# A graph layer's gathers: fewer buffers, later release in the start, and end parts placed by hand

## The chip, the cores and the metric

One core of a Trainium2 chip runs the whole program. The metric is the time of one execution on the device in microseconds, as the median over several runs; lower is better. The engines are TensorE (PE, with its weight loads as PEld), VectorE (DVE), ScalarE (ACT), GpSimd (POOL) and SyncE (SP). SP does no arithmetic here; it issues DMAs. POOL does nothing but issue indirect DMAs, the gathers.

## The reference, cut to what matters

```python
# x: 12500 x 64; src, dst: 200000 (sorted by dst); edge_attr: 200000 x 64; dist: 200000 x 1
nodes = x[stack([src, dst], 1)].reshape(200000, 128)
gates = (ssp(edge_attr @ We1 + be1) @ We2 + be2) * (1 - sigmoid(5 * (dist - 3.5)))
h     = ssp(nodes @ Wn1 + bn1) @ Wn2 + bn2
sums  = zeros_like(x).at[dst].add(h * gates)
new   = x + ssp(sums @ Ws1 + bs1) @ Ws2 + bs2
out   = layernorm(x + new)          # ssp(v) = softplus(v) - log 2, all in float32
```

## The kernel before, in words

The edges are cut into 391 groups of 512. For each group the kernel needs the rows `x[src]` of its edges. Four gathers on POOL bring them, 128 rows each, into a buffer `xg` (`gather`, L183). In twelve groups SP fetches the last 128 rows one by one instead (`fetch`, L198), so those groups have three gathers. The other half of a node product, `x[dst] @ Wn1`, is not gathered: since the edges are sorted by `dst`, the destinations of 256 edges lie within 42 neighbouring nodes, and the kernel first writes a table of all nodes' products to HBM and later loads 42 rows of it (`load`, L211). One-hot columns (`onehot`, L216), written by DVE into the same `xg` buffer, pick the right row.

**The start.** POOL issues the gathers of the first groups at once; `src` is the only thing that they need. Meanwhile constants and the transposed `x` are loaded. Then the table is made in 14 pieces: for each, PE multiplies (L501), ACT and DVE each copy a part from PSUM to `tb` (L503, L504), SP stores it, DVE clears a part of `sums` (L506). PE has two PSUM buffers for the pieces, so it is at most two ahead of the copies. After each piece stands one call of `gather(g, after=True)`: DVE writes one element of the `xg` buffer (L178), and POOL's gather of that group must wait for that write. Engines work through their queues in the order of the program, so a gather that waits holds back all later gathers, and nothing else.

**The loop.** The order of the work is written by hand (`tc.manual_schedule()`); each engine takes its own instructions in this order. In iteration i, PE does the first part of layer 2 for group i-1 (L266, L269), layer 1 for group i+1 (L233, L235, L241), the scatter of group i-3 (L292), the transposes of group i+3 (L224) and the rest of layer 2 for group i-1 (L275). ACT does exponential and logarithm of group i+1 (L252, L255) and copies the transposed rows (L229). DVE multiplies the messages (L284, L288), adds the scattered sums into `sums` (L308), takes the softplus (L260) and writes one-hots. SP loads group i+5 and fetches single rows. POOL's part is one call, `gather(i + AHEAD - 1)`. The pool has `AHEAD + 5` = 25 buffers `xg`. A gather can go as soon as its buffer is free, and that is when the scatter of the group 25 before has been done by PE; POOL, which has no other work, then takes it at once.

**Node blocks.** Whenever the sums of a block of 512 nodes are complete, its output is computed in ten parts (`node_block`): fetch of `x`, `hidden` with `clamp`, `logs`, `center`, `ssp`, `layer2` with `add`, `square`, `variance`, `root`, `scale`, `store`. `BLOCK_STEPS` says how many iterations after completion each part stands; the third row is for a block that completes close to the end.

**The end.** From iteration `ends = last - CATCH_UP` on, the loop has another branch: transposes are done for the next group only, and twice a later stage does two groups in one iteration (`second`, `third`), so that the pipeline runs empty. The last two groups and the last block follow the loop in an order written out by hand.

Of the kernel before, what the change touches and what calls it, by code (L numbers as in the profile page):

```python
# [42 lines left out]
F32 = mybir.dt.float32  # L43
# [19 lines left out]
PIECES = 3  # L63
NB = 512
K = 4
AHEAD = 20
LOADS = 5
SPREADS = 5
CATCH_UP = 17
PREPARE = 5  # L70

BLOCK_STEPS = ((2, 3, 4, 4, 6, 7, 8, 9, 10, 14), (2, 3, 3, 4, 5, 6, 7, 8, 9, 10), (1, 1, 1, 2, 3, 3, 4, 4, 4, 4))
ROWS = 4
CUTOFF = 5.0
EPS = 1e-5
# [28 lines left out]
def gnn_resnorm_kernel(ctx: ExitStack, tc: tile.TileContext, a: dict, out: bass.AP, E: int):  # L104
# [67 lines left out]

    def gather(g, after=False):

        xg = loads.tile([P, K, P], F32, name="xg", bufs=AHEAD + 5)
        xgs[g] = xg
        if after:
            nc.vector.memset(xg[:, 0, :1], 0.0)  # L178
        for k in range(K - (g in by_rows)):
            if padding(g, k):  # L180
                nc.vector.memset(xg[:, k, :D], 0.0)
                continue
            nc.gpsimd.indirect_dma_start(  # L183
                out=xg[:, k, :D], out_offset=None, in_=x,
                in_offset=bass.IndirectOffsetOnAxis(ap=src_i[:, g, k : k + 1], axis=0))
# [68 lines left out]
    def logs(g, part=every):  # L254
        nc.scalar.activation(us[g][:, part], us[g][:, part], AF.Ln, bias=one)  # L255
# [47 lines left out]
    def window(g):  # L303
        if g not in window_at:
            window_bases(g)
        for h in range(2):
            part = sums[h * D : (h + 1) * D, bass.ds(window_at[g][h], W)]
            nc.vector.tensor_add(part, part, scs[g][h * D : (h + 1) * D, h * W : (h + 1) * W])  # L308
# [89 lines left out]
    with tc.manual_schedule():  # L398
# [4 lines left out]
        with tc.tile_pool(name="prep", bufs=1) as prep:  # L403
# [15 lines left out]
            nc.sync.dma_start(dist, a["dist_l"])  # L419
            dst_i = rel.bitcast(I32)  # L420
            nc.sync.dma_start(dst_i.rearrange("p g k -> p (g k)"), a["dst_l"])
            FREE = AHEAD - 2 * PARTS
            for g in range(FREE):
                gather(g)

            nc.vector.memset(one, 1.0)
            nc.vector.memset(half, 0.5)
# [68 lines left out]
            for i in range(PARTS):  # L496
                for c in range(i * CP, (i + 1) * CP, CP // 2):
                    m = CP // 2
                    ps = z_tile().rearrange("p b (k f) -> p (b k) f", k=K)
                    for k in range(m):  # L500
                        nc.tensor.matmul(ps[:, k, :], xT[:, c + k, :], wnb, start=True, stop=True)  # L501
                    tb = prep.tile([P, m, 2 * D], F32, name="tb", bufs=6)
                    nc.scalar.copy(tb[:, :K, :], ps[:, :K, :])  # L503
                    nc.vector.tensor_copy(tb[:, K:, :], ps[:, K:m, :])  # L504
                    nc.sync.dma_start(by_node[:, c : c + m], tb)
                    nc.vector.memset(sums[:, c * P : WIDE if c + m == NCH else (c + m) * P], 0.0)  # L506
                    gather(FREE + c // m, after=True)
                if i == 1:
                    nc.vector.tensor_copy(base_i, base_b[:1])
                    for k in range(2):  # L510
                        nc.vector.tensor_copy(be3[:, k, :], rows[:, 0, :])
                    for k in range(K):
                        nc.vector.tensor_copy(row3[:, :, k, :], rows[:, 1:3, :])
                        nc.vector.tensor_copy(rs3[:, k, :], rows[:, 3, :])
                if i == 2:
                    nc.vector.tensor_copy(rel, dst_i)
                    for t in range(2):
                        r = rel[:, :, 2 * t : 2 * t + 2]
                        nc.vector.tensor_sub(r, r, base_b[:, :NH].rearrange("p (g h) -> p g h", h=2))


        with tc.tile_pool(name="finish", bufs=1) as finish:
# [5 lines left out]
            def lagging(i, lag, steps):  # L528

                lag -= sum(i > step for step in steps)  # L530
                return [g for g in range(i - lag, i - lag + 1 + (i in steps)) if g >= 0]

            for i in range(-3, NG):
                second[i] = lagging(i, 1, (ends + 5,))
                third[i] = lagging(i, 3, (ends - 2, ends + 8))
                ahead[i] = [i + 3] if i < ends else [i + 2] if i == ends + 1 else [i + 1] if i > ends + 2 else []
            parts, begun, complete = {}, None, 0

            def at(f, g, *more):
                if 0 <= g < NG:  # L540
                    f(g, *more)
# [5 lines left out]
            for i in range(-3, last - 1):  # L547
                now = parts.pop(i, [])
                early = [part for part in now if part.tensor]
                at(load, i + LOADS)  # L550
                fetch(i)
                if i > 0:
                    at(gather, i + AHEAD - 1)
                if i < ends:
                    for g in second[i]:
                        layer2_edge(g)
                    if i >= -1:
                        zs[i + 1] = z_tile()
# [12 lines left out]
                    for g in second[i]:  # L571
                        layer2_node(g)
                    for g in second[i]:
                        hcut(g)
                        message(g)
                    for g in third[i]:
                        window(g)
                    for part in early:
                        part.others()
                    at(softplus, i + 1)  # L580
                else:
                    for g in ahead[i]:
                        transposes(g)
                        xcopy(g)
                    zs[i + 1] = z_tile()
                    layer1_edge(i + 1)
                    for part in early:
                        part.tensor(zs[i + 1][:, 1, HE:])
                    layer1_node(i + 1)
                    exps(i + 1)  # L590
                    logs(i + 1)
                    for g in second[i]:
                        layer2(g)
                        hcut(g)
# [12 lines left out]
                complete = third[i][-1] + 1 if third[i] else 0  # L607
                if blocks and complete >= blocks[0][1] - PREPARE and not begun:
                    begun = node_block(*blocks[0][0], finish)
                    begun.pop(0).others()  # L610
                if blocks and complete >= blocks[0][1]:
                    steps = next(steps for steps in BLOCK_STEPS if i + steps[-1] < last - 1)
                    for n, part in zip(steps, begun, strict=True):
                        parts.setdefault(i + n, []).append(part)
                    blocks.pop(0)
                    begun = None
            assert len(blocks) == 1 and begun and not parts
# [8 lines left out]
            for some in (edge, node):  # L626
                exps(last, some)
                logs(last, some)
            for g in range(last - 2, last + 1):
                window_bases(g)  # L630
            layer2(last - 1)
# [5 lines left out]
            scatter(last - 1, tx_tile()[:, : 2 * W])  # L637
            softplus(last, node)
            window(last - 2)
            layer2_node(last)  # L640
            window(last - 1)
            hcut(last)
            message(last)
            scatter(last, tx_tile()[:, : 2 * W])
            window(last)
            for part in begun:
                node_part(part)

# [146 lines left out]
```

## Time and profile before

| | us |
|---|---|
| median of 3 runs | 2539.01 |
| lowest, highest | 2535.73, 2542.47 |
| the profiled execution's own time | 2535.25 |
| its span, from the first to the last instruction | 2533.4 |
| mean granted TensorE clock in it | 0.866 |

The profile's page gives for each group of instructions its line, engine, output and input, count, busy time, mean duration and the idle time ahead of it with what ended it. The timeline gives the start, the duration, the engine and line, and in brackets how long the engine had been idle and who released it; "remote" and "issue" are cases in which the trace names nobody. Row counts (x4) say that neighbouring equal instructions were merged. Tables by stretch give, for each engine, busy time and count, then the granted clock, the share of the DMA engines in use and GB/s.

### The profile page before, as it was taken

The numbers are of one execution on the slowest core, as the hardware profiler recorded it, in microseconds if no ns is written. First come the engines' busy times: TensorE is split into PE (matmuls) and PEld (weight loads), VectorE is DVE, ScalarE is ACT, GpSimd is POOL, SyncE is SP. The second block draws the span as 40 slices with busy tenths as digits, with TensorE's granted clock in tenths as the row PEclk, the third lists the DMA queues.
The fourth block names the chain that finished last, engine by engine and source line by source line (L and its number), as shares of the span: only waits on it lengthen the run. The fifth ranks groups of instructions, "written<-read, shape, count | busy, mean of one in ns | idle before, by whom it ended". The sixth has DMA issues, their size and how long they took to land. (4 is left out here: it accounts for less than half of the span.)

```text
span 2533.4 us, 41076 instructions
## 1 busy us (share of the span) xinstructions
PE 2139.0 (84%) x11373; PEld 1735.4 (69%) x11373; DVE 1085.8 (43%) x2745; ACT 920.1 (36%) x1317; POOL 1469.2 (58%) x1555
## 2 busy tenths in 40 slices
PE   4569888988988888888879987988898889888897
PEld 3457676777767767667767766766777667766775
DVE  3224434444444444444444444444444444444553
ACT  1123333333333333333333433333434333333442
POOL 6655666666666666656666655566666666666400
PEclk9998889788888888888997888888888888899895
DMA  7312222222222222222222222222222222222210
GB/s 194 90 45 52 51 50 53 51 51 53 51 55 50 53 52 55 53 52 57 51 55 56 50 53 53 52 57 52 57 54 53 56 54 57 55 61 55 54 48 8
DMA packets 170982, 143.07 MB, mean 56 GB/s; under 512 B 46475, under 2 KB 142915, under 8 KB 170746
## 3 DMA queue, kind: packets, MB, share of 16 engines
q1 hardware_dynamic: 119746, 87.95, 12.0%
q0 software_dynamic: 49632, 50.92, 11.2%
q8 instruction: 93, 1.52, 0.3%
q10 hardware_dynamic: 1368, 1.51, 0.2%
q14 instruction: 143, 1.17, 0.1%
HBM read 130.57 MB, written 9.63 MB: 55 GB/s over the span
## 5 line engine op out<-in xcount | busy, mean ns | idle before, releaser
L183 POOL DMA_INDIRECT xg<-in_x,src_i x1551 | 1469.0, 947 | 919.4 <-issue 361.1
L252 ACT ACTIVATE u<-z 128x768 f32<-128x768 f32 x392 | 317.0, 809 | 1435.7 <-PE z L241 469.1
L284 DVE TENSOR_TENSOR h<-gh,cut 128x256 f32<-128x256 f32 x391 | 165.9, 424 | 1162.9 <-PE z L241 369.9
L241 PE MATMUL z<-xT,wns 106*128 106x256 f32 x1564 | 497.2, 448 | 7.1 <-issue 3.2
L275 PE MATMUL gh<-consts,s 128*128 128x64 f32 x3128 | 428.9, 284 | 7.0 <-issue 6.9
L269 PE MATMUL gh<-consts,s 128*128 128x128 f32 x1564 | 310.5, 326 | 141.7 <-issue 124.1
L275 PEld LDWEIGHTS gh<-consts,s 128*128 128x128 f32 x3128 | 423.6, 210 | 4.8 <-issue 4.8
L241 PEld LDWEIGHTS z<-xT,wns 106*128 106x128 f32 x1564 | 353.1, 228 | 78.7 <-issue 8.5
L269 PEld LDWEIGHTS gh<-consts,s 128*128 128x128 f32 x1564 | 229.0, 211 | 248.7 <-issue 222.7
L260 DVE SCALAR_TENSOR_TENSOR s<-u,z 128x768 f32<-128x768 f32 x392 | 372.7, 951 | 47.6 <-issue 26.2
L255 ACT ACTIVATE u<-u,one 128x768 f32<-128x768 f32 x392 | 365.9, 933 | 12.7
L224 PE MATMUL tx<-consts,xg 128*106 128x128 f32 x1552 | 278.4, 307 | 62.8 <-ACT u L255 29.4
L235 PE MATMUL z<-eT,consts 128*128 128x256 f32 x782 | 314.7, 489 | 0.0
L292 PEld LDWEIGHTS z<-xg,msg 128*128 128x128 f32 x1484 | 272.0, 227 | 47.5 <-issue 16.1
L292 PE MATMUL z<-xg,msg 128*128 128x84 f32 x1484 | 257.0, 298 | 21.1 <-issue 20.7
L224 PEld LDWEIGHTS tx<-consts,xg 128*106 128x106 f32 x1552 | 209.9, 160 | 86.6 <-issue 38.2
L229 ACT COPY xT<-tx 106x512 f32<-106x512 f32 x391 | 221.4, 566 | 35.9 <-PE tx L224 18.5
L308 DVE TENSOR_TENSOR sums<-sums,z 64x42 f32 x742 | 145.8, 197 | 129.1 <-issue 113.9
L288 DVE TENSOR_TENSOR msg<-gh,h 128x256 f32<-128x256 f32 x391 | 165.9, 424 | 13.4
L235 PEld LDWEIGHTS z<-eT,consts 128*128 128x128 f32 x782 | 131.9, 212 | 54.9 <-issue 16.1
L266 PE MATMUL gh<-row,ones 3*128 3x512 bf16 x391 | 156.9, 401 | 3.3 <-issue 2.5
L216 DVE TENSOR_TENSOR xg<-consts,rel 128x168 f32<-128x168 f32 x391 | 135.9, 348 | 0.2
(100 smaller groups left out, 635.7 us busy)
## 6 DMA issues: line engine op xcount, KB each, us to landing
eT<-in_eT SPq DMA_DIRECT2D x391, 128.0 KB
xg<-in_x,src_i POOLq DMA_INDIRECT x1551
xr<-in_x SPq DMA_DIRECT2D x1536, 0.2 KB
wns<-table SPq DMA_DIRECT2D x782, 21.0 KB
table<-tb SPq DMA_DIRECT2D x14, 448.0 KB
sums<-in_xT SPq DMA_DIRECT2D x7, 455.0 KB
y<-in_x SPq DMA_DIRECT2D x24, 128.0 KB
out<-y SPq DMA_DIRECT2D x24, 128.0 KB
```

Of the source, the lines that this page charges most:

```text
L183: nc.gpsimd.indirect_dma_start(out=xg[:, k, :D], out_offset=None, in_=x, in_offset=bass.IndirectOffsetOnAxis(ap=src_i[:, g, k : k + 1], ax ...
L224: nc.tensor.transpose(tx[:, k, :], row, ident)
L229: nc.scalar.copy(xT, xTs[g])
L235: nc.tensor.matmul(zs[g][:, 0, :HE], we1.rearrange("a h d -> a (h d)"), eTs[g], start=False, stop=True, skip_group_check=True)
L241: nc.tensor.matmul(zn, wns[:, g % REST, h, :], xTs[g][:, h], start=True, stop=True, skip_group_check=True)
L252: nc.scalar.activation(us[g][:, part], z_of(g)[:, part], AF.Exp)
L255: nc.scalar.activation(us[g][:, part], us[g][:, part], AF.Ln, bias=one)
L260: nc.vector.scalar_tensor_tensor(ss[g].rearrange("p i t e -> p (i t e)")[:, part], us[g][:, part], BIG, z_of(g)[:, part], OP.min, OP.max)
L269: nc.tensor.matmul(v[:, 0, t], ss[g][:, 0, t, :], we2, start=False, stop=False, skip_group_check=True)
L275: nc.tensor.matmul(ghs[g][:, 1, 2 * t + h, :], ss[g][:, 1 + h, t, :], wn2, start=False, stop=h == 1 and t == 1, skip_group_check=True)
L284: nc.vector.tensor_mul(hs[g], ghs[g][:, 1], cut[:, g, :].to_broadcast([P, K, D]))
L292: nc.tensor.matmul(sc, msgs[g][:, 2 * t : 2 * t + 2, :].rearrange("p h f -> p (h f)"), xgs[g][:, 2 * t : 2 * t + 2, D:DW], start=t == 0, s ...
```

## The change

- 20 buffers `xg` instead of 25: `AHEAD` is 16, and the pool has `AHEAD + BEHIND` of them, with `BEHIND` = 4.
- In the start, groups 0 to 6 are gathered at once (before: 0 to 5). Groups 7 to 15 follow the table: three groups after every five pieces (pieces 0, 1, 3, 5, 6, 8, 10, 11 and 13), where before one group followed each piece (groups 6 to 19).
- In the loop, iteration i calls `gather(i + AHEAD)`. In iterations 0 to 3, for groups 16 to 19, the gather also waits for a DVE write at the head of the iteration; before, groups 20 to 24 had a fresh buffer and waited for nothing.
- `CATCH_UP` is 10 instead of 17: the other branch begins at iteration 380 instead of 373, and the doubled steps move with it (layer 2 from iteration 378 to 383, scatter from 371 and 381 to 378 and 385).
- A block that completes close to the end has its parts 1, 2, 1, 2 and 3 iterations later (hidden and clamp, logs, center, ssp, layer 2 and add) instead of 1, 1, 1, 2, 3; its square, variance, root, scale and store, before 3 and 4 iterations later, now stand at fixed places in the code behind the loop.

```diff
-AHEAD = 20
+AHEAD = 16
-CATCH_UP = 17
+CATCH_UP = 10
+FREE = 7
+BEHIND = 4
-BLOCK_STEPS = (..., (1, 1, 1, 2, 3, 3, 4, 4, 4, 4))
+BLOCK_STEPS = (..., (1, 2, 1, 2, 3))
...
-        xg = loads.tile([P, K, P], F32, name="xg", bufs=AHEAD + 5)
+        xg = loads.tile([P, K, P], F32, name="xg", bufs=AHEAD + BEHIND)
...
-            FREE = AHEAD - 2 * PARTS
-            for g in range(FREE):
-                gather(g)
+            waiting = {}
+            for g in range(AHEAD):
+                if g < FREE:
+                    gather(g)
+                else:
+                    waiting.setdefault(min(5 * (g - FREE) // 3, 2 * PARTS - 1), []).append(g)
...
-                    gather(FREE + c // m, after=True)
+                    for g in waiting.get(c // m, []):
+                        gather(g, after=True)
...
-                second[i] = lagging(i, 1, (ends + 5,))
-                third[i] = lagging(i, 3, (ends - 2, ends + 8))
+                second[i] = lagging(i, 1, (ends + 3,))
+                third[i] = lagging(i, 3, (ends - 2, ends + 5))
...
-                if i > 0:
-                    at(gather, i + AHEAD - 1)
+                if i >= 0:
+                    at(gather, i + AHEAD, i < BEHIND)
...
-                    for n, part in zip(steps, begun, strict=True):
+                    for n, part in zip(steps, begun):
                         parts.setdefault(i + n, []).append(part)
+                    rest = begun[len(steps) :]
...
+            square, variance, root, scale, store = (part.others for part in rest)
+            square()
...
             window(last - 2)
+            variance()
+            root()
             layer2_node(last)
             window(last - 1)
...
             window(last)
+            hidden, clamp = begun.pop(0)
+            hidden(gh_tile())
+            scale()
+            clamp()
+            store()
             for part in begun:
                 node_part(part)
```

More of the change, by code (lines that the diff above doesn't have):

```diff
@@ L65 @@
 K = 4
-AHEAD = 20
+AHEAD = 16
 LOADS = 5
 SPREADS = 5
-CATCH_UP = 17
+CATCH_UP = 10
 PREPARE = 5
-BLOCK_STEPS = ((2, 3, 4, 4, 6, 7, 8, 9, 10, 14), (2, 3, 3, 4, 5, 6, 7, 8, 9, 10), (1, 1, 1, 2, 3, 3, 4, 4, 4, 4))
+FREE = 7
+BEHIND = 4
+BLOCK_STEPS = ((2, 3, 4, 4, 6, 7, 8, 9, 10, 14), (2, 3, 3, 4, 5, 6, 7, 8, 9, 10), (1, 2, 1, 2, 3))
 ROWS = 4
@@ L533, in gnn_resnorm_kernel @@
             for i in range(-3, NG):
-                second[i] = lagging(i, 1, (ends + 5,))
-                third[i] = lagging(i, 3, (ends - 2, ends + 8))
+                second[i] = lagging(i, 1, (ends + 3,))
+                third[i] = lagging(i, 3, (ends - 2, ends + 5))
                 ahead[i] = [i + 3] if i < ends else [i + 2] if i == ends + 1 else [i + 1] if i > ends + 2 else []
-            parts, begun, complete = {}, None, 0
+            parts, begun, complete, rest = {}, None, 0, []
             def at(f, g, *more):
```

## The prediction

> **What bounds the kernel.** I read the page first. No engine is full:
>
> ```profile
> PE 2139.0 (84%) x11373; PEld 1735.4 (69%) x11373; DVE 1085.8 (43%) x2745; ACT 920.1 (36%) x1317; POOL 1469.2 (58%) x1555
> L183 POOL DMA_INDIRECT xg<-in_x,src_i x1551 | 1469.0, 947 | 919.4 <-issue 361.1
> ```
>
> A gather takes 0.94 us and the next starts 0.30 us later, so POOL is taken for longer than its 58%. The timeline of POOL and that of ACT, in the middle of the loop, show how:
>
> ```profile
> 641.40 0.94 POOL L183 DMA_INDIRECT xg<-in_x,src_i  x1 [1.36 <-PE z L235]
> 645.14 0.94 POOL L183 DMA_INDIRECT xg<-in_x,src_i  x1 [0.30 <-issue]
> 647.43 0.94 POOL L183 DMA_INDIRECT xg<-in_x,src_i  x1 [1.35 <-PE z L235]
> ...
> 647.20 0.81 ACT L252 ACTIVATE u<-z 128x768 f32<-128x768 f32 x1 [3.79 <-PE z L235]
> ```
>
> Four gathers start 1.25 us apart (641.40 to 645.14), 5.0 us for a group; then POOL waits for PE. ACT waits for PE too, and is let go at 647.20, just when POOL is (647.43), 1.1 us after the last gather ended (646.08). I read it so: while gathers follow each other without a pause (a burst), PE's signals reach the others late, and they arrive when the burst is over. POOL takes every buffer the moment PE frees it, so a round is one burst of 5.0 us and 1.0 us in which the signals pass. The starts of ACT's exponential, one for each group (two for the last), counted by stretches, give the round:
>
> ```profile
> 161.60:2385.10 2223.50, 295.81 (x365) 0.86 0.23 54
> 2385.10:2409.00 23.90, 4.05 (x5) 0.93 0.18 48
> ```
>
> 365 rounds with gathers take 6.092 us each; after the last gather, five rounds take 4.78 us each. The share of the granted clock is the first number behind the count (0.86, 0.93).
>
> The same reading, at the start. ACT's copies of the 14 table pieces (L503) and its first exponentials (L252), then POOL's gathers around the pauses:
>
> ```profile
> 41.33 0.58 ACT L503 COPY tb<-z 128x512 f32<-128x512 f32 x1 [7.89 <-remote]
> 45.96 0.58 ACT L503 COPY tb<-z 128x512 f32<-128x512 f32 x1 [2.51 <-PE z L501]
> 48.95 0.58 ACT L503 COPY tb<-z 128x512 f32<-128x512 f32 x1 [2.40 <-issue]
> 59.38 0.58 ACT L503 COPY tb<-z 128x512 f32<-128x512 f32 x1 [9.85 <-remote]
> 84.47 0.58 ACT L503 COPY tb<-z 128x512 f32<-128x512 f32 x1 [4.18 <-remote]
> 102.82 1.07 ACT L503 COPY tb<-z 128x512 f32<-128x512 f32 x2 [17.77 <-remote]
> 107.44 0.58 ACT L503 COPY tb<-z 128x512 f32<-128x512 f32 x1 [3.55 <-PE z L501]
> 116.67 0.81 ACT L252 ACTIVATE u<-z 128x768 f32<-128x768 f32 x1 [3.96 <-PE z L233]
> 144.05 0.81 ACT L252 ACTIVATE u<-z 128x768 f32<-128x768 f32 x1 [18.32 <-remote]
> 153.60 0.81 ACT L252 ACTIVATE u<-z 128x768 f32<-128x768 f32 x1 [0.47 <-PE z L241]
> 161.70 0.81 ACT L252 ACTIVATE u<-z 128x768 f32<-128x768 f32 x1 [5.85 <-PE z L292]
> ...
> 3.38 1.08 POOL L183 DMA_INDIRECT xg<-in_x,src_i  x1 [2.92 <-DMA src_i<-in_src_l]
> 39.00 0.95 POOL L183 DMA_INDIRECT xg<-in_x,src_i  x1 [0.30 <-issue]
> 43.73 0.94 POOL L183 DMA_INDIRECT xg<-in_x,src_i  x1 [3.78 <-DVE xg L178]
> 74.48 0.94 POOL L183 DMA_INDIRECT xg<-in_x,src_i  x1 [5.28 <-DVE xg L178]
> 98.20 0.94 POOL L183 DMA_INDIRECT xg<-in_x,src_i  x1 [0.30 <-issue]
> 105.22 0.94 POOL L183 DMA_INDIRECT xg<-in_x,src_i  x1 [6.07 <-DVE xg L178]
> 143.90 0.94 POOL L183 DMA_INDIRECT xg<-in_x,src_i  x1 [0.31 <-issue]
> 161.93 0.94 POOL L183 DMA_INDIRECT xg<-in_x,src_i  x1 [17.09 <-PE tx L224]
> ```
>
> ACT's long waits end when bursts end: 41.33 after 39.95, 102.82 after 99.14, 144.05 as the burst of 105.22 to 144.84 runs out. Early in a burst the pieces still pass: in the one from 43.73 the copies of 45.96 and 48.95 keep their pitch of 3.0 us, the next (due at 52.0) comes at 59.38. In the one from 74.48 a copy due at 82.8 comes at 84.47, the next at 102.82. So some 8 to 10 us are free, and then little moves until POOL pauses. The start ends at 161.93, where the gather of group 25 finds the first freed buffer and the rounds begin.
>
> The end, by stretches (the last columns are granted clock, DMA share, GB/s), and the place where the clock drops for good:
>
> ```profile
> 2409.00:2477.40 68.40, 64.56 (x392) 48.35 (x391) 39.16 (x105) 32.92 (x49) 0.00 (x0) 0.97 0.15 44
> 2477.40:2533.40 56.00, 42.02 (x140) 30.47 (x140) 18.40 (x57) 12.26 (x23) 0.00 (x0) 0.50 0.03 9
> ...
> 2476.60 0.42 ACT L346 ACTIVATE l_s<-l_s 128x256 f32<-128x256 f32 x1 [2.20 <-DVE l_s L342]
> 2478.08 2.07 PE L241 MATMUL z<-xT,wns 106*128 106x256 f32 x4 [2.39 <-ACT xT L229]
> ```
>
> A node block's logarithm waits on ACT for DVE's clamp, the next group's copy of xT stands behind it, PE idles 2.39 us, and the last 56 us run at half clock.
>
> **The change, in three terms.** The profiled span is 161.9 (start) + 2223.5 (365 rounds) + 148.0 (from the gather of the last group) = 2533.4 us.
>
> *Start.* Now 20 buffers, so the rounds begin with the gather of group 20, not 25: five groups of 5.0 us less in bursts. Seven groups go free instead of six, so the first burst runs to about 45.0 instead of 39.95 and piece 1 is copied at 46.4 (1.4 later, as before): a loss of 5.1 us. From there three groups (15.0 us of POOL) follow five pieces (15.0 us at their free pitch of 3.0); before it was five groups, 25 us, so POOL was always behind its releases and made bursts of 25 us. Twelve more pieces at 3.0 us give 82.4. The groups that follow on neighbouring pieces (10 and 11, 13 and 14) still make bursts of 10 us or a little more; at that age a copy came 1.7 us late, at 15.6 us 7.4 late. I take 2.5 us for each of the two: last piece at 87.4, say 88, instead of 107.44. The first exponential came 9.2 us after the last piece (116.67), and I keep that. Then groups 16 to 19 are each released by a DVE memset at the head of iterations 0 to 3. That memset stands in DVE's queue behind the softplus and the one-hot of the iteration before, and nothing on DVE waits behind it; POOL's queue holds only gathers, and group 16 is first used 13 iterations later. So POOL issues one group an iteration instead of eight in a row.
>
> ```profile
> 43.40 0.06 DVE L178 MEMSET xg<- 128x1 f32 x1
> ```
>
> The memset costs 0.06 us, as today's. These iterations run at half clock: 8.1 us each (153.60 to 161.70), where the stalls are gone. Start: 88 + 9.2 + 4 x 8.1 = 130. From below: 20 groups are 100 us, the first issue 3.4, and the three pauses before group 20 were 3.8 + 5.3 + 6.1: 119. From above: the table no quicker than before, 107.4 + 9.2 + 32.4 = 149. I take 130, nearer to the low end, since that is where group 20 stood already in the row of 105.22 (twelve gathers later, 120.3).
>
> *Rounds.* Groups 20 to 390 go through 370 rounds instead of 365. POOL's lead of 17 iterations instead of 22 hides the landing of a gather either way; the round is the burst plus the hand-over, and neither has changed. 370 x 6.092 = 2254.0, which is 30.5 more.
>
> *End.* Five groups fewer are left when the last gather goes out: 148.0 - 23.9 = 124.1. Catching up begins at iteration 380 instead of 373. Seven catch-up iterations become plain ones, which I cost at nothing: PE is busy 64.56 of 68.40 us in one kind and about as densely in the five plain rounds. The double steps are as many as before, later. The block's logarithm now stands one iteration behind its clamp, so the 2.39 us go, and what is late next is the double scatter and the block's sums, gaps of about 1 us that stay. Square, variance, root, scale and store move behind the loop. On ACT the square and the root no longer delay two copies of xT. On DVE the variance falls into the first of these waits, beside PE work; the others are the costs as the last block's rows and the loop's show them:
>
> ```profile
> 2514.89 0.42 DVE L308 TENSOR_TENSOR sums<-sums,tx 64x42 f32 x2 [1.54 <-PE tx L292]
> 2525.03 0.42 ACT L366 ACTIVATE y<-y 128x256 f32<-128x256 f32 x1 [2.23 <-DVE y L362]
> 2525.48 0.42 DVE L370 TENSOR_REDUCE var<-y 128x4 f32<-128x256 f32 x1 [0.48 <-ACT y L366]
> 2485.80 0.16 DVE L380 TENSOR_SCALAR scaled<-var 128x4 f32<-128x4 f32 x1
> 2486.59 0.42 DVE L384 TENSOR_TENSOR y<-y,rstd 128x256 f32<-128x256 f32 x1
> ```
>
> The square is 0.42, the variance 0.42 in a wait of 1.54. The five instructions of scale (2485.80 to 2487.01, 1.2 us) run beside the last block's matmuls; without that cover they would cost those 1.2. The store is one issue on SP that stands ahead of the final store with all its loads done. The unknown is the clock. PE is busy for 42.02 us at half clock; if all of it ran at full speed that would save 21. If the clock falls at the double steps and stays down, nothing is saved, or 3 lost. I take 10, about half: 114, with ends at 100 and 127.
>
> Sum: 130 + 2254 + 114 = 2498 us of span, against 2533.4. The profiled execution's time was 1.85 above its span, and the median of the runs 3.8 above that: 2504.
>
> **A rule against it.** In the stretch of bursts the table's stores, eT loads and gathers use the same engines. The Trainium skill, DMA: Bandwidth & Descriptors, section SWDGE vs HWDGE vs iDMA, says that each DMA engine has 16 queues, that POOL's and SP's DMAs feed different ones, and that the engine goes round them in turn. By that rule a burst can't shut out the others, and spacing it out would win nothing. The rows of ACT's waits speak against it as the whole story; they do not say which path is blocked.
>
> **Rivals.** *The start isn't shortened* (something else than bursts holds it). For it: the waits are put down to "remote", with no name. Then the start is the upper end, 149, the end 124.1: 2527 of span, 2533 as a median, within 0.3% of now.
>
> *The clock holds at the end.* The gap of 2.39 us stands right ahead of the drop; without it the last 56 us go faster by the full 21: 2487 of span, 2493. The Trainium skill, TensorE: Matmul & The Clock Gate, section Part 1, says that one busy window of about 3.4 us brings full clock back and an idle one takes it; by that rule the end is this rival's. The row of 56 us at 0.50 with 42 us of busy PE agrees badly with it.
>
> *Slower: every burst, however short, holds PE's signals to its end.* Then groups 8 to 15 go one after another: 5.0 of burst, 2.3 until the signal (1.4 to 3.7 above), 2.4 from copy to gather (41.33 to 43.73), 9.7 each, and the last piece comes at about 46.4 + 7.5 x 9.7 = 119. Four loop iterations, each of 5.0 + 1.1 and some 3.2 from exponential to release, add 37, with 9.2 before them: 165. Span 165 + 2254 + 124 = 2543, median 2549. It decides once the start is longer than 163. Against it: the copies of 45.96 and 48.95 inside a burst.
>
> **How the numbers follow.** 0.3% (7.6 us) is about what a measurement can tell from no change. Forecast 0.57, clock holds 0.18, start not shortened 0.16, slower 0.09. The first two and nearly half of the third are faster: 0.82; the rest of the third is the same, 0.09. Forecast and clock together span 119 + 2254 + 100 to 149 + 2254 + 124; with 5.6 on top, and the low corner cut where both unknowns would have to fall well, the range is 2482 to 2532.
>
> **What would show it.** Right: ACT's last L503 copy near 88, no wait of 10 us on ACT in the start, the gather of group 20 near 130, then 6.09 us a round; the last gather near 2384 and 114 us behind it; no 2.39 us gap ahead of L241. Wrong: pieces that still wait 10 us although POOL pauses, or a round longer than 6.1.

## The result: 2483 us instead of 2541, 2.3% faster

| | before | after |
|---|---|---|
| median, us (4 runs each) | 2540.74 | 2483.28 |
| lowest to highest | 2535.73 to 2545.99 | 2475.08 to 2485.62 |
| profiled execution's own time; span | 2535.25; 2533.4 | 2482.05; 2480.3 |
| mean granted TensorE clock | 0.866 | 0.861 |
| start + rounds + end, us | 161.9 + 2223.5 + 148.0 | 126.4 + 2253.6 + 100.3 |

The ratio is 0.977 (95% interval 0.974 to 0.980). The forecast was 2504 us, 0.986 of the time before: the sign was right, the gain was 57 us where 35 had been forecast, and the time lies at the very bottom of the range. On two later visits to a chip the changed kernel was 48.3 and 46.2 us faster (0.980 and 0.981, intervals 0.977 to 0.984 and 0.978 to 0.984). So a part of the 57 seems to belong to the runs, not to the change.

On some visits to a chip the kernel before takes about 2500 us in all its runs (state A: the prediction, its result and all that follows unless it says B), and on others about 2000 (state B).

The page of the changed kernel has the same load on every engine (PE 2139.0, POOL 1469.2 before):

```profile
PE 2138.7 (86%) x11373; PEld 1741.1 (70%) x11373; DVE 1087.5 (44%) x2744; ACT 920.1 (37%) x1317; POOL 1473.3 (59%) x1555
```

In sum no engine has less work; what changed is where the waits lie and at which clock the end runs. The start, by the timelines of ACT (copies of the table's pieces L510, exponentials L255) and of POOL (first gathers after a pause):

```profile
33.92 0.59 ACT L510 COPY tb<-z 128x512 f32<-128x512 f32 x1
41.30 0.59 ACT L510 COPY tb<-z 128x512 f32<-128x512 f32 x1 [6.80 <-remote]
53.99 1.07 ACT L510 COPY tb<-z 128x512 f32<-128x512 f32 x2 [12.10 <-remote]
58.61 0.59 ACT L510 COPY tb<-z 128x512 f32<-128x512 f32 x1 [3.55 <-PE z L508]
...
73.54 0.59 ACT L510 COPY tb<-z 128x512 f32<-128x512 f32 x1 [2.40 <-PE z L508]
79.74 0.59 ACT L510 COPY tb<-z 128x512 f32<-128x512 f32 x1 [5.61 <-PE z L508]
...
87.35 0.59 ACT L510 COPY tb<-z 128x512 f32<-128x512 f32 x1 [2.40 <-PE z L508]
...
99.34 0.81 ACT L255 ACTIVATE u<-z 128x768 f32<-128x768 f32 x1 [6.72 <-PE z L238]
...
122.13 0.81 ACT L255 ACTIVATE u<-z 128x768 f32<-128x768 f32 x1 [4.54 <-PE gh L278]
...
133.82 0.81 ACT L255 ACTIVATE u<-z 128x768 f32<-128x768 f32 x1 [7.52 <-PE gh L278]
```

```profile
49.05 0.95 POOL L186 DMA_INDIRECT xg<-in_x,src_i  x1 [0.30 <-issue]
57.73 1.08 POOL L186 DMA_INDIRECT xg<-in_x,src_i  x1 [7.74 <-DVE xg L181]
...
82.13 0.94 POOL L186 DMA_INDIRECT xg<-in_x,src_i  x1 [2.31 <-DVE xg L181]
102.64 0.94 POOL L186 DMA_INDIRECT xg<-in_x,src_i  x1 [5.82 <-DVE xg L181]
116.38 0.94 POOL L186 DMA_INDIRECT xg<-in_x,src_i  x1 [3.99 <-DVE xg L181]
134.06 0.95 POOL L186 DMA_INDIRECT xg<-in_x,src_i  x1 [2.98 <-PE gh L278]
```

The first burst ends at 50.0 us (the first line of POOL), and pieces 2 and 3 come at 53.99, after a wait of 12.10: the prediction's sign "no wait of 10 us on ACT in the start" did not come true. From 58.61 on the pieces come every 2.99 us, but for one wait of 5.61, and the last is at 87.35 instead of 107.44. POOL now waits for DVE, where it used to be behind. The burst from 116.38 runs into group 20 (its first gather starts at 126.38); in it one exponential comes 11.7 us after the one before (122.13 to 133.82), and ACT is idle for 7.52 of them. Before, the one such wait was 18.32.

The rounds, by the exponentials counted from the gather of group 20 (126.38) to that of group 390 (2379.95; the stretch below is put 0.2 us later), and the end, by stretches that part where the granted clock falls for the last time; then PE's two longest waits in the end before that fall:

```profile
126.60:2380.20 2253.60, 299.87 (x370) 0.85 0.23 54
```

```profile
2373.50:2465.70 92.20, 86.16 (x545) 68.10 (x544) 55.48 (x150) 44.94 (x69) 6.62 (x7) 1.00 0.14 37
2465.70:2480.30 14.60, 4.15 (x12) 2.50 (x11) 4.70 (x17) 1.84 (x5) 0.00 (x0) 0.50 0.08 23
...
2439.52 0.62 PE L227 MATMUL tx<-consts,xg 128*106 128x128 f32 x4 [1.31 <-issue]
2452.98 0.74 PE L361 MATMUL z<-consts,l_s 128*128 128x128 f32 x4 [2.02 <-DVE l_s L353]
```

2253.60 / 370 is 6.091 us a round, as before. The last 14.6 us run at half clock; before it was the last 56.0. The wait of 2.39 us ahead of layer 1 is gone. One of 2.02 has come: layer 2 of the block that completes close to the end waits for that block's `ssp`, which now follows a later logarithm (before, this wait was 0.42). Here it did not take the clock.

### The profile page after: what moved, and what is told of

It reads as the page before. It is cut to its first block, busy times and chain, and to the rows that moved or that the text cites. A ratio compares the mean times of both kernels' runs of the same rounds, so it can differ in the third digit from the quotient of the medians.

```text
span 2480.3 us, 41084 instructions
## 1 busy us (share of the span) xinstructions
PE 2138.7 (86%) x11373; PEld 1741.1 (70%) x11373; DVE 1087.5 (44%) x2744; ACT 920.1 (37%) x1317; POOL 1473.3 (59%) x1555
## 4 chain that ended last, share of the span: by engine, by line
PE 79%; issue 9%; DVE 5%; ACT 3%; another core or an unknown queue 3%; DVEq 1%; DMA 1%; SPq 0%; ACTq 0%
PE z L244 17%; PE gh L278 12%; PE gh L272 11%; PE z L238 11%; PE tx L227 8%; PE z L295 8%; PE gh L269 4%; PE z L236 3%; PE tx L330 2%; DVE h L287 1%; DVE msg L291 1%; ACT u L255 1%; DVE sums L311 1%; PE z L508 1%
## 5 line engine op out<-in xcount | busy, mean ns | idle before, releaser
L255 ACT ACTIVATE u<-z 128x768 f32<-128x768 f32 x392 | 317.4, 810 | 1435.4 <-PE z L244 466.8
L295 PEld LDWEIGHTS z<-xg,msg 128*128 128x128 f32 x1512 | 279.8, 230 | 41.1 <-issue 8.2
L295 PE MATMUL z<-xg,msg 128*128 128x84 f32 x1512 | 263.4, 301 | 14.5 <-issue 14.2
## 6 DMA issues: line engine op xcount, KB each, us to landing
eT<-in_eT SPq DMA_DIRECT2D x391, 128.0 KB
y<-in_x SPq DMA_DIRECT2D x24, 128.0 KB
out<-y SPq DMA_DIRECT2D x24, 128.0 KB
```

The source lines that it names most:

```text
L255: nc.scalar.activation(us[g][:, part], z_of(g)[:, part], AF.Exp)
L295: nc.tensor.matmul(sc, msgs[g][:, 2 * t : 2 * t + 2, :].rearrange("p h f -> p (h f)"), xgs[g][:, 2 * t : 2 * t + 2, D:DW], start=t == 0, s ...
```

## Experiments

"Theory" is that of the prediction: bursts of gathers hold PE's signals back, and the end is set by the gaps that take the clock. Kernels under one heading ran together and share the runs of the kernel before.

### Start and end alone

The kernel before took 2512.7 us here (median of 27 runs, 2490.6 to 2526.3).

**The new end alone** (start, 25 buffers and the loop's gathers as before):

```diff
-CATCH_UP = 17
+CATCH_UP = 10
 ... BLOCK_STEPS, second, third and the parts behind the loop as in the change
```

> The kernel before with the end of the changed one (catch-up from iteration 380, the shorter steps of a late block, parts behind the loop placed by hand); start and buffers as before. Theory (the end parts keep the clock up): start 161.9 and 365 rounds stay, the end falls from 148.0 to about 124 (its 100.1 in the changed kernel plus 23.9 for five groups more), so 24 us less than before, about 2516. Rival (the end of the changed kernel was short because its gathers run later, not because of its end parts): 0 to 5 us less than before.

Measured: 2495.8 us, ratio 0.993 (0.990 to 0.997), 16.9 us faster, where 24 had been expected. Its last term is 124.3 us, against 145.2 in the kernel with the logarithm moved alone, the third one here; no trace of the kernel before was taken on this visit.

**The new start alone** (20 buffers, three groups behind five pieces, the loop's wait for DVE; the end as before):

```diff
-AHEAD = 20
+AHEAD = 16
+FREE = 7
+BEHIND = 4
 ... gather, waiting and the loop's call as in the change
```

> The kernel before with the start and the 20 buffers of the changed one; end as before. Theory: start near 126.6, 370 rounds of 6.09 = 2253.6, end 148.0 - 23.9 = 124.1, with the clock falling for good near its end as before: 29 us less than before, about 2511. Rival (later gathers keep the clock up in the end by themselves): 50 us less, like the changed kernel.

Measured: 2492.3 us, ratio 0.993 (0.990 to 0.996), 20.4 us faster, where 29 had been expected. By its trace the start is 127.3 us (156.7 in the next kernel), the rounds 370 x 6.014, the last term 123.3. So the start is 29.4 us shorter, five rounds more take 30 back, and the last term, with five groups fewer, gives 21.9 (the prediction had 23.9). The two parts are worth about the same and add up to 37.3; on other visits the whole change gave 46 to 57, and it did not run on this one.

**The logarithm's place alone**, in the kernel before:

```diff
-BLOCK_STEPS = (..., (1, 1, 1, 2, 3, 3, 4, 4, 4, 4))
+BLOCK_STEPS = (..., (1, 2, 1, 2, 3, 3, 4, 4, 4, 4))
```

> The kernel before with one number changed: the logarithm of a block that completes late stands two iterations after completion instead of one; all else as before. Theory (PE's wait of 2.39 us behind that logarithm is what drops the clock): the wait goes, the last 56 us run mostly at full clock, 15 to 21 us less than before. Rival (the double steps or the other late parts drop it): 2 to 5 us less.

Measured: 2512.6 us, ratio 0.999 (0.996 to 1.002): nothing. The wait of 2.39 us is gone from its trace, and the clock falls at another place, at a wait of 2.01 us, 46 us before the end:

```profile
2453.00:2499.40 46.40, 33.13 (x111) 24.36 (x111) 14.22 (x43) 9.30 (x18) 0.00 (x0) 0.50 0.04 10
...
2453.31 1.22 PE L358 MATMUL z<-consts,l_s 128*128 128x128 f32 x4 [2.01 <-DVE l_s L350]
```

So taking this gap away only hands the clock to the next one, and the same move makes that one: layer 2 of the block now waits 2.01 us, where it waited 0.42.

**The changed kernel with the logarithm back**, one iteration after the clamp's:

```diff
-BLOCK_STEPS = (..., (1, 2, 1, 2, 3))
+BLOCK_STEPS = (..., (1, 1, 1, 2, 3))
```

> The changed kernel with that one number put back: logarithm one iteration after completion, all else as changed. Theory: a wait of about 2.4 us on PE comes back and the clock falls behind it, 12 to 20 us more than the changed kernel. Rival: only the 2.4 us come back, or nothing.

Measured: 2480.1 us, ratio 0.987 (0.982 to 0.991). The changed kernel did not run beside it; start and end alone would give 2475.4. Its trace has the wait of 2.39 us, and the clock falls there for good:

```profile
2415.20:2460.80 45.60, 33.08 (x112) 24.63 (x112) 15.47 (x49) 9.54 (x19) 0.00 (x0) 0.50 0.04 10
...
2415.38 2.07 PE L244 MATMUL z<-xT,wns 106*128 106x256 f32 x4 [2.39 <-ACT xT L232]
```

Its last term is 114.2.

### Beside the changed kernel

The kernel before: 2541.9 us (11 runs, 2529.5 to 2551.7).

**The changed kernel again.**

> The changed kernel itself, unchanged, to stand beside three edits of it on one chip. In the traces so far the start (to the gather of the first reused buffer) is 160.2 and 156.9 us with the old start and 127.4 and 127.3 with the new, and the end is 145.2 with the old, 124.3 with the new end and 25 buffers. If these terms carry the change, this run has a start of 127, rounds of 6.00 to 6.09 us by the chip, an end of 100 to 105, and a time 2.0% to 2.4% under the kernel before, whatever chip it is. If the gain is particular to the first chip (the rival: start and end alone gave 0.7% each elsewhere), it is 1.3% to 1.6%.

Measured: 2493.6 us, ratio 0.980 (0.977 to 0.984). Terms: 128.0 + 370 x 6.117 + 106.9. The start is as expected; rounds and end are a little over what was (6.09 and 105). The 57 us of the first visit are above what others gave.

**The logarithm back, again.**

> The changed kernel with the last blocks' logarithms one iteration after hidden and clamp, as before, instead of two; run a second time, now beside the changed kernel. In its first profile the end was 114.2 us, PE had the gap of 2.39 us at 2413 us, and the granted clock fell there to 0.50 and stayed. Theory (the gap takes the clock, and with the parts behind the loop nothing brings it back): the end is 12 to 16 us longer than in the changed kernel beside it, the median 10 to 16 us. Rival (the clock falls wherever it falls, gap or not): medians within 5 us, and a profile in which the clock's last fall does not stand at that gap.

Measured: 2496.5 us, 2.9 more than the changed kernel, where the theory wanted 10 to 16: the rival's size, and the runs of the two overlap. But the trace has the theory's mechanism: the clock falls at the wait of 2.39 us, and stays down for 20.5 us. In the changed kernel beside it, it fell at the wait of 2.01 us, and stayed down for the last 31.7:

```profile
2454.74 2.07 PE L244 MATMUL z<-xT,wns 106*128 106x256 f32 x4 [2.39 <-ACT xT L232]
```

```profile
2464.45 0.74 PE L361 MATMUL z<-consts,l_s 128*128 128x128 f32 x4 [2.01 <-DVE l_s L353]
```

Last terms: 109.4 and 106.9. In that execution the changed kernel lost almost as much at another gap.

**No wait for DVE in the loop:**

```diff
-                    at(gather, i + AHEAD, i < BEHIND)
+                    at(gather, i + AHEAD)
```

> The changed kernel, but groups 16 to 19 in the loop's first four iterations wait for nothing but POOL's queue. Theory (bursts hold PE's signals back): groups 14 to 19 make one burst of about 30 us right when the loop begins, the first exponentials wait in it for more than 10 us, and the start is 3 to 12 us longer. Rival (the wait for DVE does nothing, since groups 18 to 20 go back to back with it too): start and median within 3 us.

Measured: 2493.2 us, the same (0.981, 0.978 to 0.984). The trace shows what the theory said: exponentials at 101.61 and 122.05, nothing between, and a start of 134.3 instead of 128.0, since POOL then waits for PE:

```profile
134.29 0.94 POOL L186 DMA_INDIRECT xg<-in_x,src_i  x1 [17.30 <-PE tx L227]
```

But 6 us can't be told by runs that scatter by 9 to 17. The wait for DVE is worth its 6 us in one trace and is not shown in the time.

**Five groups free, 18 buffers:**

```diff
-AHEAD = 16
+AHEAD = 14
-FREE = 7
+FREE = 5
```

> The changed kernel with five groups gathered at once instead of seven, AHEAD 14 and 18 buffers; nine groups follow the table as before. Theory: the first burst is two groups (10 us) shorter, so table, first exponential and start come 10 us earlier; two rounds more (12 us) and two plain rounds fewer behind the last gather (9.6 us); 7 us faster in sum. Rival: the table cannot begin earlier than its inputs and the start gains 5 us or less, so that the sum is between 2 us faster and 3 us slower; and if a lead of 14 iterations is too short for a landing, the rounds get longer than those of the changed kernel.

Measured: 2491.6 us, ratio 0.979 (0.975 to 0.983), 2.0 under the changed kernel: not told apart. By its trace the start is 7.6 us shorter (120.3), two rounds more cost 10.7, the last term is 7.3 less.

### Bursts, in state B

The kernel before took 2012 us here (one run). Four edits of the changed kernel that were to test the bursts:

```diff
 all free:            -FREE = 7
                      +FREE = 16
 all behind the table: min(5 * (g - FREE) // 3, 2 * PARTS - 1)  ->  2 * PARTS - 1
 one behind a piece:   ...  ->  min(g - FREE, 2 * PARTS - 1)
 three gathers:        padding(g, k) is also true for k >= 3
```

> The changed kernel with all first 16 groups gathered at once, so that POOL issues 63 gathers without a pause from 3.3 us to about 83. Theory (a burst holds PE's signals until it ends): the pieces of the table, apart from the first few, wait until the burst is over; the last piece comes near 122 instead of 87, the first exponential near 134 instead of 99, the start is 155 to 165 instead of 127. Rival (the engines go round the queues in turn, a burst shuts nobody out): the pieces go on at about 3 us through the burst, the last is not later than 95, and the start not longer than 135.

> The changed kernel with all nine later groups (7 to 15) released after the last piece, so that the table is made while POOL pauses, and a burst of 45 us stands where the loop begins. Theory (bursts): the pieces keep their pitch of 3.0 us once the first burst is over, the last at about 80; then some 8 to 10 us are free, so that one or two exponentials come near 90 to 95, and no more until the burst ends near 125. Rival: the table is no quicker than in the changed kernel (87), and the exponentials go on through the burst, one every 6 to 8 us.

> The changed kernel with three gathers for each group instead of four; the fourth 128 rows are filled with zeros by DVE, so that part of the messages is left out. Theory (a round is one burst and a hand-over): 3 x 1.25 + 1.0 is 4.8 us, which is also the 4.78 us of the rounds without gathers; rounds of 4.8 to 5.0 us, a span of about 2000 to 2070. Rival (the round is PE's work at a clock that falls now and then, and POOL only fits in): rounds of 5.7 to 6.1 us, a span over 2340.

> The changed kernel with groups 7 to 15 released one behind each of the pieces 0 to 8, as the kernel before did, instead of three after every five pieces. Theory (a group of 5.0 us after each piece of 3.0 us leaves POOL behind its releases, and bursts form): the table is held in bursts of 20 us and more, the last piece comes between 92 and 102 instead of 87, the start is 5 to 12 us longer. Rival (seven groups at once and 20 buffers are all that counts): last piece at 85 to 89 and the same start, 127.

Measured, as time; start; round: all free 2002.1; 109.0; 4.973. All behind the table 2033.0; 139.2; 4.976. One behind a piece 1996.5; 107.0; 4.976. Three gathers 1852.1; 98.6; 4.453, each one run. Here no burst held anything back. With all free, POOL issues without a pause from 3 us on; the pieces keep their pitch of 2.99 us, and the exponentials follow:

```profile
37.34 0.58 ACT L510 COPY tb<-z 128x512 f32<-128x512 f32 x1 [3.55 <-PE z L508]
...
70.20 0.58 ACT L510 COPY tb<-z 128x512 f32<-128x512 f32 x1 [2.40 <-PE z L508]
...
78.35 0.81 ACT L255 ACTIVATE u<-z 128x768 f32<-128x768 f32 x1 [2.96 <-PE z L244]
82.38 0.81 ACT L255 ACTIVATE u<-z 128x768 f32<-128x768 f32 x1 [1.78 <-PE z L244]
```

The theory fails in all four: a burst shuts nobody out here, as the first rival said. The numbers of the other rivals are not met either, since table and start were quicker than they had (last pieces at 71 to 72 us, starts under 127 but for the second kernel). A round is just POOL's own four gathers, 4.97 us, without a hand-over. With three gathers PE is the bound (4.45 us a round, PE 97% busy).

### The same, in state A

The kernel before: 2535.3 us (8 runs).

> The changed kernel itself. If the kernel before takes 2490 to 2550 us on this visit (state A, rounds of 6.0 to 6.1 us): start 125 to 129, end 99 to 108, 1.9% to 2.4% faster. If it takes about 2012 (state B, rounds of 4.98 us, the four gathers' own pitch): theory, the change saves what the start saves when nothing is held back, with the rounds bound by POOL's gathers from the first to the last: 16 to 18 us fewer by what POOL no longer waits in the start, the end about the same, so 0 to 20 us faster. Rival in state B: the fewer buffers cost as much as the start gains, within 5 us.

Measured: 2489.1 us, ratio 0.981 (0.978 to 0.984). Terms 127.8 + 370 x 6.100 + 102.7.

> The changed kernel with all first 16 groups gathered at once, so that POOL issues 63 gathers without a pause from 3.3 us to about 83. In state A, theory (a burst holds PE's signals back until it ends): the last piece of the table near 122 instead of 87, the first exponential near 134 instead of 99, start 155 to 165 instead of 127, span 25 to 40 us over the changed kernel. Rival: pieces at about 3 us through the burst, start under 135. In state B it did the second (start 109.1, first exponential 78.5), and would do so again.

Measured: 2517.2 us, 28.1 over the changed kernel; start 157.7. The burst held the table from 53.69 to 90.09, 5.6 us after its last gather had ended (84.53), and from 94.71 on the pieces ran at 2.99 us with POOL silent:

```profile
53.69 0.59 ACT L510 COPY tb<-z 128x512 f32<-128x512 f32 x1 [20.86 <-remote]
90.09 0.59 ACT L510 COPY tb<-z 128x512 f32<-128x512 f32 x1 [35.81 <-remote]
...
121.59 0.59 ACT L510 COPY tb<-z 128x512 f32<-128x512 f32 x1 [2.40 <-PE z L508]
...
83.59 0.94 POOL L186 DMA_INDIRECT xg<-in_x,src_i  x1 [0.30 <-issue]
132.20 0.95 POOL L186 DMA_INDIRECT xg<-in_x,src_i  x1 [47.67 <-DVE xg L181]
```

The same can be seen in one stretch inside the burst. The columns are busy time and count of PE, PEld, DVE, ACT and POOL, then granted clock, DMA share and GB/s; first state A, then the same kernel in state B:

```profile
60.00:84.00 24.00, 0.00 (x0) 0.00 (x0) 0.00 (x0) 0.00 (x0) 18.21 (x20) 1.00 0.15 26
```

```profile
58.00:84.00 26.00, 23.32 (x92) 19.28 (x91) 9.14 (x17) 7.89 (x12) 19.59 (x22) 1.00 0.50 156
```

In state A PE, DVE and ACT stand still, and the DMA engines are busy for 0.15 of the time, at 26 GB/s. So it is not their transfer rate that runs short; in state B they move 156 GB/s beside the same gathers.

> The changed kernel with groups 7 to 15 all released after the last piece. In state A, theory: the last piece near 80, one or two exponentials near 90 to 95, then none until the burst of 45 us ends near 125; start about 150. Rival: exponentials every 6 to 8 us through the burst. In state B it had its first exponential at 80.0 and a start of 139.6, and would again.

Measured: 2505.5 us, 16.4 over the changed kernel; start 154.0. Groups 16 and 17 joined the burst, so it runs from 79.75 to 134.37. Two exponentials come within 10 us of its beginning, then none for 40 us:

```profile
79.75 0.94 POOL L186 DMA_INDIRECT xg<-in_x,src_i  x1 [40.22 <-DVE xg L181]
133.43 0.94 POOL L186 DMA_INDIRECT xg<-in_x,src_i  x1 [0.30 <-issue]
...
85.10 0.81 ACT L255 ACTIVATE u<-z 128x768 f32<-128x768 f32 x1 [2.60 <-issue]
...
89.76 0.81 ACT L255 ACTIVATE u<-z 128x768 f32<-128x768 f32 x1 [2.42 <-PE z L238]
...
130.40 0.81 ACT L255 ACTIVATE u<-z 128x768 f32<-128x768 f32 x1 [31.62 <-remote]
```

The hold is not strict: this third one comes 4 us before the burst's end, as the copy at 53.69 in the kernel above came in the middle of one.

> The changed kernel with three gathers for each group instead of four (the fourth 128 rows are filled with zeros by DVE, that part of the messages is left out). In state A, theory (a round is one burst and a hand-over of 1.0 us): rounds of 4.8 to 5.0 us. Rival (PE's work at a clock that falls now and then): rounds of 5.7 to 6.1. In state B it had rounds of 4.45 us, PE's own, at a granted clock of 0.995.

Measured: 2130.7 us (one run), mean round 5.186. The median round is 4.66 (six rounds from 999.43 to 1027.44 take 4.67 each), as 3 x 1.25 and a hand-over of 0.9:

```profile
999.43 0.94 POOL L186 DMA_INDIRECT xg<-in_x,src_i  x1 [1.15 <-PE gh L278]
1000.67 0.95 POOL L186 DMA_INDIRECT xg<-in_x,src_i  x1 [0.30 <-issue]
1001.93 1.09 POOL L186 DMA_INDIRECT xg<-in_x,src_i  x1 [0.30 <-issue]
1004.12 0.94 POOL L186 DMA_INDIRECT xg<-in_x,src_i  x1 [1.10 <-PE tx L227]
...
1027.44 0.95 POOL L186 DMA_INDIRECT xg<-in_x,src_i  x1 [1.10 <-PE z L236]
```

The mean lies between the theory's 4.8 to 5.0 and the rival's 5.7 to 6.1, nearer to the theory. It is the weakest of the tests, since PE's own round in state B is 4.45, only 0.2 below the median. The two edits of the start carry the argument: in state A both agree with the bursts of the prediction. One behind a piece did not run in this state, so what it is worth to release three groups after five pieces, and not one after each, was not tried apart.

### State B again, and fewer gathers

The kernel before: 2019.1 us (11 runs).

> The changed kernel itself. If the kernel before takes 2490 to 2550 us on this visit: 1.9% to 2.4% faster, start 125 to 129, rounds 6.00 to 6.12, end 99 to 108. If it takes about 2012: 0 to 20 us faster.

Measured: 1995.9 us, ratio 0.989 (0.986 to 0.992), 23 us faster, a little more than expected. POOL issues without a pause up to the end of the rounds (1838.60 us for 370, 4.969 each). There is no trace of the kernel before in this state, so where the 23 us come from was not shown.

**Eight single rows an iteration on SP**, so that 24 groups have three gathers, not 12 (1539 gathers in the trace, not 1551):

```diff
-ROWS = 4
+ROWS = 8
```

> The changed kernel with ROWS 8 instead of 4: SP fetches eight single rows an iteration instead of four, so that every 16th group, not every 32nd, has three gathers: 23 groups instead of 12, the same work in all. Theory (a round is its gathers, 1.25 us each, and a hand-over): 11 or 12 gathers fewer, 14 us faster than the changed kernel beside it; with the 0.91 us that one gather was worth in the test before, 10. Rival (SP's issues, 3.75 us of a round now and some 5.5 then, become late, and eT and wns with them): 0 to 30 us slower. In the state of 2012 us, where the gathers' own pitch is the round, the theory gives the same 14 us.

Measured: 2539.5 us, 544 us slower than the changed kernel beside it. The rival's mechanism at many times its price: in 23 rounds, one for nearly every group with single rows, PE stood still and the round took 19 to 25 us, some 390 us of the 544. The waits of its transposes (us in total, times, the longest):

```profile
PE tx L227 <- DMA xr<-in_x: 180.3, 13, 15.8
PE tx L227 <- DMA wns<-table: 147.5, 11, 15.9
```

Between those waits the exponentials came 4.35 us apart for the most part. SP did not bring twice the single rows in time; whether fewer gathers make the round shorter is told by the kernel with three gathers alone.

## The prediction, step by step

**The reading: bursts hold PE's signals back.** That a burst holds the other engines back is right for state A, by an experiment that could have refuted it (pieces held from 53.69 to 90.09). That it is PE's signals, and not something else that comes late, was argued and not shown. "8 to 10 us are free" was right too: exponentials 5.4 and 10.0 us into the burst of 79.75, the next 40 us later. It is not a law of the program: in state B nothing is held. There the prediction's reading, its 6.09 us a round and its start would all have been wrong. The rule that the prediction set against itself, the Trainium skill, DMA: Bandwidth & Descriptors, section SWDGE vs HWDGE vs iDMA (a DMA engine goes round its queues in turn), agrees with state B (pieces every 2.99 us while POOL issues without a pause) and not with state A.

**Start, 130.** 126.4, then 128.0 and 127.8. The last piece was forecast at 88 and came at 87.35, by luck in part. The first burst ran to 50.0, not 45.0: piece 1 was copied at 41.30, inside it, not at 46.4, and so released group 8 into it. That put the pieces about 3 us behind the forecast's pitch; the later bursts then cost 2 us, not 5. Behind the table two more steps were off and cancelled: the first exponential came 12.0 us after the last piece, not 9.2; and the four iterations took 6.8 us each ((126.38 - 99.34) / 4), not 8.1, because groups 18 to 20 went out back to back, not one an iteration.

**Rounds, 370 x 6.092 = 2254.0.** 2253.6. Leads of 17 or 15 iterations were as good as 22, as the kernel with 18 buffers also shows (6.113 beside 6.117).

**End, 114: the step that failed.** 100.3, the low end of its bounds; 106.9 and 102.7 later. The 23.9 us for five groups were right within 2 (145.2 to 123.3 is 21.9). What was mis-sized is the clock's share: "I take 10, about half". The new end alone measured 20.9 us (145.2 to 124.3) in the traces and 16.9 in the median, near the full 21 that the prediction had as a bound and gave to its rival, "the clock holds".

The traces tell how much of it is the clock. Four matmuls of layer 1 take 2.07 us at half clock (at 2478.08 in the kernel before) and 1.03 at full:

```profile
2421.64 1.03 PE L241 MATMUL z<-xT,wns 106*128 106x256 f32 x4
```

So half of PE's busy time at half clock is what the clock costs; this is an estimate. In the kernel before it is 24.4 us of the end's 148.0, in the changed kernel 2.2 in the first trace, 10.2 and 5.2 in the two later ones: 14 to 22 us less, where 10 was taken. With this cost taken off, the end is 123.5 us in the kernel before, 119.1 in the new end alone, 102.3 in the new start alone, and 96.7 to 98.3 in all eight traces of state A with the new end and 20 buffers. So the new end itself saves 4 to 6 us, which the prediction put at next to nothing, and the clock makes the rest.

The cause that the prediction named was too narrow as well: the gap of 2.39 us alone is worth nothing (0.999) in the kernel before, and 3 us by the median, not clear of the noise, in the changed one. It expected gaps of about 1 us next, and a wait of 2.0 came, which took the clock in both later traces (for the last 31.7 us in one) and not in the first. What seems to count is that the catch-up begins later and the last block's parts stand behind the loop, so that less work is left after the last fall. How much each of these two gives was not tried apart.

**The sum.** The span came out 17.7 us under the forecast: 3.6 start, 0.4 rounds, 13.7 end. Most of the rest of the 20.7 is that the median of the four runs lay 3.0 above the span, not 5.65.

**Rivals.** "The start isn't shortened" fell with 126.4; "slower" needed a start of over 163. "The clock holds at the end", 2493, was nearest to the median: the later visits gave 2489 and 2494.

## What to carry to other kernels

When one engine issues DMAs without a pause, look at what the others wait for at that time, not at its busy share; here the place of nine groups of gathers was worth 16 to 28 us, with every engine's work the same. Where the clock fell at a gap, removing that gap did not win it back: look for the next one of more than 1 us, and shorten what runs behind the last. Before two versions are compared to 0.3%, run them side by side: the kernel before took 2490.6 to 2526.3 us within one visit, its median moved by 29 us between visits of state A, and by 500 between the states.

## What the hardware showed that was not expected

**Two states.** One program takes 2500 us on one visit and 2000 on another, on the same chips, and mixes within a visit were not seen. In state A PE's matmuls also wait with no releaser that the trace names ("issue"), in B hardly. The row of layer 2's matmuls (busy time, mean ns, then idle time ahead of them and what ended it), state A (the changed kernel again), then B (the changed kernel again, there):

```profile
L272 PE MATMUL gh<-consts,s 128*128 128x128 f32 x1564 | 308.4, 325 | 123.9 <-issue 113.2 <-DVE s L263 9.8
```

```profile
L272 PE MATMUL gh<-consts,s 128*128 128x128 f32 x1564 | 280.3, 302 | 0.0
```

What sets the state stays open. That instructions, and not only signals, come late behind a burst would fit these rows, and no run tried it. The trace with all groups free speaks against it in part: its packets of the kind "instruction" show none between 54 and 96 us, and yet the table goes on at 90.09.

**When the clock falls.** I counted PE's idle time (between matmuls) in each unit of 3.41 us of the clock's records, in five traces of state A (the kernel before, the changed kernel on three visits, the first one with the logarithm back), from 300 us on. At full clock, of 1717 units with less than 0.9 us idle 12 were followed by half clock; of 516 with 0.9 to 1.7 us, 349; of 70 with more, 69. At half clock, full speed came back after 417 of 660 units with less than 0.1 us idle, and after 9 of 243 others. So a gap of 1.3 to 2 us takes the clock or does not, by how the unit's border cuts it. The wait of 2.02 us in the changed kernel's profile leaves 0.9 us in one unit and 1.2 in the next, and the clock stays; the one of 2.01 us in the changed kernel again leaves 0.7 and 1.3, and the clock falls; with the logarithm moved alone it leaves 1.5 in one unit, and the clock falls. This fits an end that varied from 100 to 107 us in one kernel. The Trainium skill, TensorE: Matmul & The Clock Gate, section Part 1, has the free-running window of 3413 ns, which agrees with the records' 3.41. Its rule that it takes an idle window to lose the clock does not agree: 0.9 to 1.7 us of idle time in a unit were enough in 349 of 516.
